# Hybrid layer stack on one core: where expert-table transfers stand among GpSimd's operations, and when the first late tiles' table rows are read

## The chip, the core and the metric

The kernel runs on one core of a Trainium2 chip. A core has five engines that run side by side, each in the order of its own instruction stream: TensorE (PE, matrix products; its weight loads are shown as PEld), VectorE (DVE), ScalarE (ACT), GpSimd (POOL) and SyncE (SP, which here only issues transfers). The engines wait for each other through semaphores. Transfers between the on-chip memory and DRAM run on 16 DMA engines; those whose rows are chosen by an index held on the chip (indirect transfers) are issued by GpSimd and occupy it for about a microsecond each, all others are issued by SyncE, in its order.

The metric is the device time of the core in microseconds, from the first instruction to the last.

## What is computed

Four layers follow each other on x, which is 2 batches of 2048 positions of 256 numbers in float32:

```python
x = L0_attn_a_u
x = x + _L0_attn_a_ref(_layernorm(x), ...)   # state space layer
x = x + _L0_ffn_ref(_layernorm(x), ...)      # experts
x = x + _L0_attn_b_ref(_layernorm(x), ...)   # attention
x = x + _L0_ffn_ref(_layernorm(x), ...)      # the same experts again
```

The state space layer, cut to what matters:

```python
zxbcdt = jnp.einsum('bld,ed->ble', u, W_in)
z = zxbcdt[..., :D_INNER]
xBC = zxbcdt[..., D_INNER:D_INNER + CONV_DIM]
dt = zxbcdt[..., D_INNER + CONV_DIM:]
xBC = jax.nn.silu(_causal_depthwise_conv(xBC, conv_w, conv_b))
x, Bm, Cm = ...                              # parts of xBC; x has 8 heads of 64
dt = jax.nn.softplus(dt + dt_bias)
A = -jnp.exp(A_log)
# for each position, per head: h = h * exp(dt * A) + (dt * x) B ; y = h C
y = _ssd_scan(dt, A, x, Bm, Cm)
y = y + D * x
y = y * jax.nn.silu(z)
y = y * lax.rsqrt(jnp.mean(y * y, axis=-1, keepdims=True) + EPS) * norm_w
return jnp.einsum('ble,de->bld', y, W_out)
```

The experts layer: each of the 4096 tokens is scored for 8 experts, the two with the highest scores are kept, and the token gets the weighted sum of those two experts' results:

```python
scores = x @ Wr.T + br
w = softmax(scores)
_, idx = jax.lax.top_k(scores + biases_N, 2)
val = w at idx, divided by its sum
h = x @ Wl1[e] + bl1[e]                      # a, b = halves of h, 512 wide each
y = (silu(a) * b) @ Wl2[e] + bl2[e]
out = sum over the two experts of val * y
```

## The kernel before

**Tiling.** The 4096 tokens are eight groups of 512 positions (`order`: the two batches in turn, place by place; a name such as f02 is the group of batch 0, place 2), and each group is four chunks of 128 (a name such as 021 is batch 0, place 2, chunk 1). The state space layer takes the 32 chunks in turn, and in each it carries the state h of the batch forward.

**Routing on the chip.** When a group's chunks are done, its tokens are scored and ranked (`prepare`), and each token gets two slots in a table in DRAM, one for each of its experts. A row of the table holds a token number, a weight and a second index. The rows are written by `enter` (L433): eight indirect transfers for each group (4 chunks by 2 experts), issued by GpSimd. Slots fill by expert, so that as soon as enough groups are entered some tiles of 256 rows of one expert are known to be full. `plan_early` works out on VectorE which those are. After groups 3, 4, 5, 6 and 7 it admits tiles up to number 5, 9, 13, 17 and 21 (`EARLY`), so that 21 "early" tiles, fe0 to fe20, are computed while the state space layer still runs. The rest, f0 and on, follow after it.

**An expert tile.** It reads its table rows (`rows`, tab_fe, L656, on SyncE), loads its expert's weights w1, w2, b1, b2 (`load`, L668 to L674, on SyncE; each has two buffers, so the load of a tile waits until the tile two before has done with them), gathers its 256 tokens (xs_fe, L683, indirect, GpSimd), transposes them (pxs_fe on PE, copied as xT_fe by ScalarE), makes four pieces of the up product (pab_fe, L722, 8 products each in two PSUM buffers; ScalarE applies silu, sa_fe L730, VectorE multiplies, gT_fe L731, which frees the PSUM buffer), the down product (pf_fe, L754), the weighting (y_fe, L767) and adds the result to the residual rows in DRAM by two indirect transfers (resid, L778, GpSimd).

**A chunk.** The loop body of the state space layer issues, for chunk i: a step of the early tile; `spread`, the load lb of chunk i+2's row of decays to all partitions (L1023, SyncE, two buffers); `chunk_front` of chunk i+1 (PE: pz, px, pb; ScalarE: eight operations lt that read lb, L1044, and an exponential; VectorE: dtx, xd, gm; GpSimd: wx L1071); a step of the early tile; `chunk_back` of chunk i (PE: py, ph, pi; GpSimd: h times its decay L1098, y+xd L1110, y*sz L1113, with VectorE's y, h+ph L1100 and y+pi L1112 between); a step of the early tile; and `chunk_out` of chunk i-1 (ScalarE: the square of y L1122; GpSimd: the inverse root ss L1124; PE: transposes pty, the output product po L1132; VectorE: x L1140). Between these stand pieces of the next group's projection (`project`: pc, pe, pd).

**Places of the transfers.** `late.step()` is called behind each of five GpSimd operations of a chunk: wx, h, y+xd, y*sz and ss. Each call lets the generator `entering` go on by one step: some empty steps, then one table transfer a step. `tc.issue_after(on_pool[0])` says that a transfer may not be issued before the GpSimd operation recorded last by `pool(...)`.

**Order.** A list scheduler of the framework decides the order of each engine's instructions in this stage [...], except for SyncE, which keeps the order of the program. So a transfer's lower bound is the operation it was called behind, and the scheduler may still put later operations of GpSimd ahead of it. In `run`, which does the tiles f0 and on, the orders of GpSimd, ScalarE and VectorE are also those of the program. After the last chunk a short loop goes on with the steps that are left, and then the late tiles begin; `fetch(tables, tiles)` reads table rows and loads weights up to the numbers given.

Of the kernel before, what the change touches and what calls it, by code (L numbers as in the profile page):

```python
# [8 lines left out]
F32 = mybir.dt.float32  # L9
# [4 lines left out]
P = 128  # L14
# [32 lines left out]
def kernel(  # L47
# [24 lines left out]
    nc = tc.nc  # L72
# [5 lines left out]
    fe = ctx.enter_context(tc.tile_pool(name="fe", bufs=2))  # L78
# [8 lines left out]
    order = [(b, s) for s in range(NS) for b in range(NB)]  # L87
# [139 lines left out]

    on_pool = []

    def pool(i):  # L230
        on_pool[:] = [i.ins]


    def layernorm(x, name):

        st = lnp.tile([P, GT, 6], F32, tag="st", name=f"st_{name}")
        mv = lnp.tile([P, GT, 2], F32, tag="mv", name=f"mv_{name}")
        for t in range(GT):
            nc.vector.bn_stats(st[:, t, :], x[:, t, :])
            nc.vector.bn_aggr(mv[:, t, :], st[:, t, :])  # L240
        yield
        rs = lnp.tile([P, GT], F32, tag="rs", name=f"rs_{name}")
        nc.vector.tensor_scalar(rs, mv[:, :, 1], EPS, None, ALU.add)
        pool(nc.gpsimd.tensor_tensor(rs, rs, mhalf, ALU.pow))
        yield
        xn = lnp.tile([P, GT, DM], F32, tag="xn", name=f"xn_{name}")
        for t in range(GT):
            nc.vector.tensor_scalar(
                xn[:, t, :], x[:, t, :], mv[:, t, 0:1], rs[:, t : t + 1], ALU.subtract, ALU.mult
            )  # L250
        return xn, rs, mv[:, :, 1]
# [24 lines left out]
    def apart(i, group, reason):  # L276
        tc.declare_no_dep(i.ins, group=group, reason=reason)
        tc.add_to_no_dep_group(group, i.ins)

    class Experts:  # L280
# [132 lines left out]
        def enter(self, pay, at, off):  # L413

            if self.rest is not None:
                rest, self.rest = self.rest, None
                for t in range(TT // P):
                    for e in range(NE):
                        with tc.issue_after(on_pool[0]):
                            i = nc.gpsimd.indirect_dma_start(  # L420
                                out=self.table,
                                out_offset=bass.IndirectOffsetOnAxis(ap=self.free[:, t, e : e + 1], axis=0),
                                in_=rest[:, t, :],
                                in_offset=None,
                            )
                        apart(i, f"free_{self.name}", "slots differ")
                        self.freed.append(i.ins)
                        if e % 2:
                            yield
            for t in range(GT):  # L430
                for c in range(2):
                    with tc.issue_after(on_pool[0]):
                        i = nc.gpsimd.indirect_dma_start(  # L433
                            out=self.table,
                            out_offset=bass.IndirectOffsetOnAxis(ap=at[:, t, c : c + 1], axis=0),
                            in_=pay[:, t, c, :],
                            in_offset=None,
                        )

                    apart(i, f"table_{self.name}", "slots differ")  # L440
                    for j in self.freed:
                        tc.add_manual_dep(
                            i.ins,
                            j.name,
                            mybir.DependencyInfo(mybir.DependencyClass.Sync, mybir.DependencyReason.DATA),
                            reason="behind the tokens that fill the first slots",
                        )
                    tc.declare_no_dep(i.ins, group=f"rows_{self.name}", reason="slots of full tiles are taken")
                    if c or not self.direct:
                        yield  # L450
# [403 lines left out]
    ffn = Experts("f", tc.dram_tile([NT + TT, DM], F32, name="resid"))  # L854
# [3 lines left out]
    with tc.tile_pool(name="ssm1", bufs=1) as s1, tc.tile_pool(name="ssm2", bufs=2) as s2:  # L858
# [170 lines left out]
        def chunk_front(b, s, t, g, lb):  # L1029
# [21 lines left out]
            for c in range(DI // P):  # L1051
# [17 lines left out]

            wx = s2.tile([P, DI], F32, tag="wx", name=f"wx_{nm}")  # L1070
            pool(nc.gpsimd.tensor_tensor(  # L1071
                wx.rearrange("p (h d) -> p h d", h=NH),
                dtxh,
# [7 lines left out]
        def chunk_back(b, s, t, g, f):  # L1081
# [14 lines left out]
            nc.tensor.matmul(ph, f["bt"], f["wx"], start=True, stop=True)  # L1096
            hh = h.rearrange("p (h d) -> p h d", h=NH)
            pool(nc.gpsimd.tensor_tensor(hh, hh, g["dec"][:, 1, t, :].unsqueeze(2).to_broadcast(per_head), ALU.mult))  # L1098
            late.step()
            nc.vector.tensor_tensor(h, h, ph, ALU.add)  # L1100
# [45 lines left out]
        late = Aside()  # L1146
# [6 lines left out]
        EARLY = {3: 5, 4: 9, 5: 13, 6: 17, 7: 21}  # L1153
# [3 lines left out]
        def routing(b, s):  # L1157
            nonlocal routed
            routed_group = yield from ffn.prepare(b, s, "B", known=True)
            routed += 1  # L1160
            late.add(entering(routed, routed_group))
            if routed + 3 < len(order):
                load_x(*order[routed + 3], x_rows(flat(u), *order[routed + 3]))


        def entering(n, group):
            if n < len(order):
                for _ in range(9 if 3 < n < len(order) - 1 else 4):
                    yield
            yield from ffn.enter(*group)  # L1170
            if n in EARLY:
                ffn.plan_early(n, EARLY[n], group[2])
# [32 lines left out]
        while late.waiting:  # L1205
            if not planned and len(ffn.seq) == EARLY[len(order) - 1]:
                ffn.plan()
                planned = True
            late.step()
            tiles.step()  # L1210
    ssm_w.__exit__(None, None, None)

    attw = ctx.enter_context(tc.tile_pool(name="attw", bufs=1))
# [3 lines left out]
    late = ffn.run()  # L1217
# [9 lines left out]
    with tc.tile_pool(name="att1", bufs=1) as a1, tc.tile_pool(name="att2", bufs=2) as a2:  # L1227
# [29 lines left out]
        EARLY = {4: 5, 6: 9}  # L1257
# [283 lines left out]
```

## Time and profile before

Times are of three runs; the profile is one more execution, whose records run over a span of 1694.1 us.

| | us |
|---|---|
| time, median of three runs | 1698.82 |
| lowest and highest | 1694.02, 1705.58 |
| profiled execution, its own time | 1695.92 |
| its span | 1694.1 |
| mean granted TensorE clock | 0.972 of full speed |

By its trace the profiled execution has these stretches:

| us from the start | what runs | PE busy, us |
|---|---|---|
| 0 to 140 | constants, first projections, first chunks | 118.53 |
| 140 to 262 | chunks; the transfers of the first two groups | 105.78 |
| 262 to 310 | chunks; the third group is entered and planned | 40.33 |
| 310 to 716 | chunks with one early expert tile beside each | 378.85 |
| 716 to 880 | late expert tiles | 159.12 |
| 880 to 920 | passage to the attention layer | 34.79 |
| 920 to 1320 | attention layer | 389.98 |
| 1320 to 1694 | experts again | 356.74 |

A stretch minus PE's busy time is what PE idled there; the waits of the trace say for what. The 64 table transfers were issued from 144.4 us to 697.6 us and took 1.13 us each on GpSimd, 72.3 us in all.

### The profile page before, as it was taken

How to read it: one execution, taken by the hardware profiler on the slowest of the kernel's cores; microseconds unless marked ns; L12 is line 12 of the kernel's file. 1: busy time of each engine (PE TensorE's matmuls, PEld its weight loads, DVE VectorE, ACT ScalarE, POOL GpSimd, SP SyncE). 2: the span in 40 equal slices, each digit the busy share in tenths (PEclk: the TensorE clock that was granted, in tenths of full speed). 3: DMA queues.
4: the chain of work that ended last, by engine and by line, in shares of the span. 5: the costliest groups of instructions: out<-in, count | busy, mean ns of one | idle time of the engine just before them, and what ended most of it. 6: DMA issues, size and time to landing. Idle time of an engine off the chain costs nothing.

```text
span 1694.1 us, 22151 instructions
## 1 busy us (share of the span) xinstructions
PE 1584.1 (94%) x7088; PEld 1193.8 (70%) x7088; DVE 897.0 (53%) x2471; ACT 670.9 (40%) x1338; POOL 736.2 (43%) x702
## 2 busy tenths in 40 slices
PE   6997988989989989999998999899999999999997
PEld 4664555677766777788885566475767878888886
DVE  6778878837648464422226757547554622222222
ACT  4886867856647543222332201101020322333322
POOL 2356357455555566634442002422240663544443
PEclk9898988999989999999999999999999999999999
DMA  4112202742535455889852231706435588888883
GB/s 157 38 54 60 88 28 61 215 126 61 168 63 160 125 144 131 209 244 320 230 133 82 54 72 52 100 13 139 144 62 150 147 215 240 222 231 229 230 215 48
DMA packets 174744, 231.30 MB, mean 137 GB/s; under 512 B 45920, under 2 KB 138080, under 8 KB 174368
## 3 DMA queue, kind: packets, MB, share of 16 engines
q1 hardware_dynamic: 143520, 193.42, 38.9%
q0 software_dynamic: 31104, 36.42, 12.0%
q8 instruction: 58, 0.95, 0.2%
q14 instruction: 62, 0.51, 0.1%
HBM read 192.72 MB, written 37.06 MB: 136 GB/s over the span
## 4 chain that ended last, share of the span: by engine, by line
PE 66%; DVE 12%; DMA 11%; POOL 5%; ACT 3%; issue 3%; SPq 1%; DVEq 0%; POOLq 0%; ACTq 0%
PE pab_g L722 9%; PE pao L1431 7%; PE pab_fe L722 5%; PE pq L1337 5%; PE pab_f L722 5%; PE pf_g L754 4%; PE pf_fe L754 4%; PE pab_ge L722 3%; DVE xc L1007 3%; PE pk L1337 3%; PE pvd L1411 3%; PE pi L1103 2%; DMA lb<-sums 2%; PE pc L990 2%; PE pf_f L754 2%
## 5 line engine op out<-in xcount | busy, mean ns | idle before, releaser
L722 PE MATMUL pab_g<-xT_g,w_g 128*128 128x256 f32 (+1 forms) x896 | 181.6, 361 | 0.0
L722 PE MATMUL pab_fe<-xT_fe,w_fe 128*128 128x256 f32 x672 | 157.8, 390 | 20.0 <-DVE gT_fe L731 17.1
L722 PEld LDWEIGHTS pab_g<-xT_g,w_g 128*128 128x128 f32 x896 | 158.5, 191 | 19.4 <-ACT xT_g L713 0.4
L722 PEld LDWEIGHTS pab_fe<-xT_fe,w_fe 128*128 128x128 f32 x672 | 128.5, 194 | 46.9 <-DVE gT_fe L731 21.8
L778 POOL DMA_INDIRECT out_dram<-y_g,tab_g x51 | 80.3, 1575 | 137.4 <-DVE y_g L767 57.9
L730 ACT ACTIVATE sa_g<-pab_g,b_g 128x256 f32<-128x256 f32 (+1 forms) x112 | 50.9, 454 | 191.3 <-PE pab_g L722 191.3
L731 DVE SCALAR_TENSOR_TENSOR gT_g<-pab_g,b_g,sa_g 128x256 f32<-128x256 f32 (+1 forms) x112 | 51.5, 460 | 129.0 <-ACT sa_g L730 129.0
L1337 PE MATMUL pq<-w_qkv_sb,axT 128*128 128x512 f32 x256 | 117.1, 597 | 0.0
L1007 DVE SCALAR_TENSOR_TENSOR xc<-pre,conv_w_sb,xc 128x512 f32<-128x512 f32 x144 | 113.3, 796 | 6.0 <-ACT xc L999 5.4
L1431 PE MATMUL pao<-w_o_sb,o 128*128 128x256 f32 x512 | 112.3, 380 | 0.0
L1431 PEld LDWEIGHTS pao<-w_o_sb,o 128*128 128x128 f32 x512 | 97.1, 190 | 15.8 <-issue 2.6
L433 POOL DMA_INDIRECT table_g<-pay_g,at_g x64 | 62.7, 980 | 86.2 <-DVE w_g L409 52.7
L990 PE MATMUL pc<-xT,w_in_sb 128*128 128x512 f32 x192 | 97.4, 638 | 0.4 <-ACT xc L999 0.4
L722 PE MATMUL pab_f<-xT_f,w_f 128*128 128x256 f32 (+1 forms) x512 | 96.6, 347 | 0.0
L754 PE MATMUL pf_g<-w_g,gT_g 128*128 128x256 f32 x408 | 92.9, 380 | 0.0
L722 PEld LDWEIGHTS pab_f<-xT_f,w_f 128*128 128x128 f32 x512 | 85.5, 191 | 9.4
L1044 ACT ACTIVATE lt<-lb,cum 128x128 f32<-128x128 f32 x256 | 82.8, 394 | 19.0 <-DMA lb<-sums 19.0
L1337 PEld LDWEIGHTS pq<-w_qkv_sb,axT 128*128 128x128 f32 x256 | 48.6, 192 | 58.8 <-issue 57.4
L1352 ACT ACTIVATE kd<-pk 128x512 f32<-128x512 f32 x32 | 19.1, 597 | 162.4 <-PE pk L1337 96.0
L778 POOL DMA_INDIRECT resid<-y_fe,tab_fe x42 | 67.0, 1595 | 37.5 <-DVE y_fe L767 21.9
L731 DVE SCALAR_TENSOR_TENSOR gT_fe<-pab_fe,b_fe,sa_fe 128x256 f32<-128x256 f32 x84 | 39.7, 480 | 80.5 <-ACT sa_fe L730 80.4
L754 PE MATMUL pf_fe<-w_fe,gT_fe 128*128 128x256 f32 x336 | 80.3, 392 | 2.2 <-DVE gT_fe L731 2.2
(477 smaller groups left out, 3368.6 us busy)
## 6 DMA issues: line engine op xcount, KB each, us to landing
w_g<-in_wl_dram SPq DMA_DIRECT2D x28, 1024.0 KB
w_fe<-in_wl_dram SPq DMA_DIRECT2D x21, 1024.0 KB
lb<-sums SPq DMA_DIRECT2D x32, 512.0 KB
w_f<-in_wl_dram SPq DMA_DIRECT2D x16, 1024.0 KB
o<-prob SPq DMA_DIRECT2D x32, 512.0 KB
w_g<-in_wl_dram SPq DMA_DIRECT2D x28, 512.0 KB
w_fe<-in_wl_dram SPq DMA_DIRECT2D x21, 512.0 KB
w_ge<-in_wl_dram SPq DMA_DIRECT2D x9, 1024.0 KB
```

Source lines behind the costliest of these rows:

```text
L433: i = nc.gpsimd.indirect_dma_start(out=self.table, out_offset=bass.IndirectOffsetOnAxis(ap=at[:, t, c : c + 1], axis=0), in_=pay[:, t, c, ...
L722: nc.tensor.matmul(p[:, q * n : (q + 1) * n], t["w1"][:, k, c * P : (c + 1) * P], t["xT"][:, k, :], start=(k == 0), stop=(k == KD - 1),)
L730: nc.scalar.activation(sa[:, :n], p[:, 0:n], AF.Silu, bias=t["b1"][:, i : i + 1])
L731: nc.vector.scalar_tensor_tensor(t["gT"][:, i, :n], p[:, n : 2 * n], t["b1"][:, NHT + i : NHT + i + 1], sa[:, :n], ALU.add, ALU.mult)
L754: nc.tensor.matmul(pos[h][:, h * DM : (h + 1) * DM], t["gT"][:, j, h * P : (h + 1) * P], t["w2"][:, j, :], start=(j == 0), stop=(j == NHT ...
L778: j = nc.gpsimd.indirect_dma_start(out=self.acc if self.direct else self.acc[: self.seq[i][4] or NT + TT, :], out_offset=bass.IndirectOffs ...
L990: nc.tensor.matmul(pc, w_in_sb[:, k, DI + c * P : DI + (c + 1) * P], xT[:, k, :], start=(k == 0), stop=(k == KD - 1),)
L1007: nc.vector.scalar_tensor_tensor(xc[:, c, :], pre[:, c, j : j + TG], conv_w_sb[:, c, j : j + 1], xc[:, c, :], ALU.mult, ALU.add,)
L1044: nc.scalar.activation(lt[:, i, :], lb[:, i, :], AF.Relu, bias=g["cum"][:, t, i : i + 1], scale=-1.0)
L1337: nc.tensor.matmul(p, src[:, k, t * P : (t + 1) * P], w_qkv_sb[:, k, j, half * TG : (half + 1) * TG], start=(k == 0), stop=(k == KD - 1),)
L1411: nc.tensor.matmul(pvd, w_qkv_sb[:, k, 2, c * P : (c + 1) * P], xd[:, k, :], start=(k == 0), stop=(k == KD - 1),)
L1431: nc.tensor.matmul(po[:, j * DM : (j + 1) * DM], o[i][:, c, (t + j) * P : (t + j + 1) * P], w_o_sb[:, c, :], start=(c == 0), stop=(c == NA ...
```

## The change

- **A fixed order on GpSimd.** Each table transfer is put into the list `in_table`. The next operation that goes through `pool(...)` is made to depend on it without a semaphore: it must stand behind it in GpSimd's stream. Together with the lower bound that was there, a transfer now stands just between two operations of the program's order. `enter` of the second experts layer (`direct`) takes no part.
- **Other holds.** `entering` waited 9 empty steps for groups 4 to 6 and 4 for groups 1, 2, 3 and 7, and none for group 8. It now waits 5, 5, 4 and 1 for groups 4, 5, 6 and 7, 3 for groups 1 to 3, and none for group 8.
- **The loop after the last chunk** takes two late steps a turn where it took one, each followed by a one-number memset on GpSimd that goes through `pool(...)`, so that the transfers have operations to stand behind.
- **Table rows of late tiles.** `fetch(25, 0)` is called at the end of the state space stage: SyncE reads the rows of the first late tiles' table (tab_f0 and on) before it loads the weights of the last early tile.

```diff
@@ pool
     on_pool = []
+    in_table = []
 
     def pool(i):
         on_pool[:] = [i.ins]
+        while in_table:
+            tc.add_manual_dep(
+                i.ins,
+                in_table.pop().name,
+                mybir.DependencyInfo(mybir.DependencyClass.NoSync, mybir.DependencyReason.DATA),
+                reason="transfers into a table keep their order",
+            )
@@ Experts.enter
                             in_=pay[:, t, c, :],
                             in_offset=None,
                         )
+                    assert self.direct or not in_table
+                    in_table.append(i.ins)
@@ entering
+        HELD = {4: 5, 5: 5, 6: 4, 7: 1}
+
         def entering(n, group):
             if n < len(order):
-                for _ in range(9 if 3 < n < len(order) - 1 else 4):
+                for _ in range(HELD.get(n, 3)):
                     yield
             yield from ffn.enter(*group)
@@ after the last chunk
             late.step()
+            pool(nc.gpsimd.memset(fe.tile([P, 1], F32, tag="sep", name="sep"), 0.0))
+            late.step()
+            pool(nc.gpsimd.memset(fe.tile([P, 1], F32, tag="sep", name="sep"), 0.0))
             tiles.step()
+        ffn.fetch(EARLY[len(order) - 1] + 4, 0)
     ssm_w.__exit__(None, None, None)
```

By the instruction orders of the two programs, a transfer stands at every one of the five places in the new one as well. TensorE, VectorE and ScalarE get a new order in the state space stage too, since the scheduler works from the new constraints: an early tile's up and down products move by a third to half a chunk against the chunk's own products. The attention layer and the second experts layer keep their orders but for a few places.

## The prediction

> **What bounds the kernel now.** I read the page first (busy shares and slices), then busy time by stretch, then the waits of the stretch that holds most of the change, then the chain of waits inside it. The page names TensorE:
>
> ```profile
> PE 1584.1 (94%) x7088; PEld 1193.8 (70%) x7088; DVE 897.0 (53%) x2471; ACT 670.9 (40%) x1338; POOL 736.2 (43%) x702
> ```
>
> GpSimd, whose order is changed, is 43% busy, so its work costs only where somebody waits for it. Busy time by stretch says where that can be; the change touches the first three rows and the first microseconds of the fourth:
>
> ```profile
> 140.00:262.00 122.00, 105.78 (x463) 68.67 (x464) 100.33 (x249) 87.39 (x172) 68.50 (x63) 0.90 0.20 57
> 262.00:310.00 48.00, 40.33 (x182) 27.07 (x180) 39.53 (x112) 34.09 (x71) 33.02 (x31) 0.89 0.26 69
> 310.00:716.00 406.00, 378.85 (x1757) 294.44 (x1757) 239.36 (x703) 218.61 (x431) 223.54 (x197) 0.97 0.51 138
> 716.00:880.00 164.00, 159.12 (x832) 141.34 (x833) 43.11 (x98) 49.91 (x114) 71.54 (x57) 0.99 0.84 244
> ```
>
> The columns are stretch and length, busy PE, weight loads, DVE, ACT, POOL, the granted clock, DMA share and GB/s. PE is idle 16.2, 7.7, 27.2 and 4.9 us. In the first two stretches DVE is nearly as busy as PE, so a delay there reaches PE through DVE. From 310 on one early expert tile (fe) runs beside each chunk, and PE alone is the bound. Its waits there, and those of the engines that feed it (us, times, longest):
>
> ```profile
> PE pab_fe L722 <- DVE gT_fe L731: 17.1, 13, 4.3
> PE pxs_fe L709 <- DMA xs_fe<-xnd_f,tab_fe: 3.8, 3, 1.6
> ACT lt L1044 <- DMA lb<-sums: 19.0, 9, 4.6
> ACT yt L1122 <- POOL y L1113: 45.0, 14, 5.6
> SPq L670 <- PE pf_fe L754: 58.5, 13, 6.5
> SPq L656 <- DMA table_f<-pay_f,at_f: 20.0, 5, 5.0
> ```
>
> Two thirds of PE's idle time is an up pass (pab) waiting for a PSUM buffer that DVE's gT has not freed. The chain of waits shows why (start, duration, what):
>
> ```profile
> 326.88 3.45 PE pf_fe L754 x16
> ...
> 331.92 6.22 DMA lb<-sums
> 338.14 0.02 issue
> 338.16 0.69 ACT lt L1044 x2
> 338.85 0.36 ACT sa_fe L730
> ...
> 475.15 8.76 DMA lb<-sums
> 483.91 0.02 issue
> 483.93 0.03 ACT lt L1044
> 483.96 0.28 issue
> 484.24 1.26 ACT lt L1044 x4
> 485.50 0.37 ACT sa_fe L730
> 485.87 0.03 issue
> 485.89 0.49 DVE gT_fe L731
> ```
>
> SyncE's queue holds the load of the next tile's w2 (L670) until this tile's down pass (pf_fe) has read the old one; the chunk's row broadcast lb stands behind it, lands 6 to 9 us later, and ScalarE, which works in order, stands on lt with sa_fe behind it. So the kernel's loss in its longest stage is the phase between a tile's down pass and the next chunk's lb.
>
> **The change part by part.** All 64 table transfers stay: their row (64 instructions, 72.3 us on POOL, 1.13 us each) is the same before and after.
>
> 1. Holds. A group's eight transfers began after 9 late steps for groups 4 to 6 and 4 for the others; now after 5, 5, 4 (groups 4, 5, 6), 1 (group 7), else 3. By the instruction orders of the two programs they stand up to one chunk earlier on POOL. What waits for them is SyncE's read of table rows: 20.0 us in 5 waits, on a queue with lb behind it. They now come ahead of lb, rather than after: 2 to 5 us each, most of it under other loads' waits.
>
> 2. Program order on POOL. Each transfer now stands between the two POOL operations of its place. It adds no POOL time, but wx, h, y+xd, y*sz or ss behind it start 1.13 us later each. At 140 to 262 POOL shows 68.50 us in 122 and its transfers are already mixed with the chunk's operations: I take 0, bounds -3 and +3 (half the 6.4 us that DVE waits there for h).
>
> 3. The first early tile. Its last transfer came at 293.7 by the trace, its table read at 298.9, its rows landed at 310.6. With the new hold I put the last transfer some 10 us earlier, and the read at about 289, behind the planning on DVE (about 4 us) that must precede it. In the new order the tile's transposes (pxs_fe0) stand before the following chunk's py, so PE waits there about 4.5 to 6 us instead of 1.05; the stage still ends earlier: -3, bounds -9 and +3.
>
> 4. The steady part, where the scheduler's order follows. An early tile moves by a third to half a chunk: its down pass now precedes py, ph and pi, where it closed the chunk before. So w2's slot comes free half a chunk earlier relative to the use of lb, and the waits on lb should go: at most the 17.1 us of PE waits, if nothing takes their place. What is late next: in the new order POOL has both scatter-adds of a finished tile (2 x 1.60 us, the resid row) ahead of h, y+xd and y*sz, and ACT has the square of y (L1122, waits for y*sz) ahead of the next sa_fe in ten passes. In a pass with three transfers POOL then runs wx 1.04, scatter-adds 3.19, h 1.18, y+xd 1.41, y*sz 1.31 and transfers 3.4 = 11.5 us in series, without transfers 8.1. PE's own work in a pass that projects nothing is pz 1.73, pab 6.9, pf 3.5, pi 1.73, py, ph 0.87 each, po 1.8, transposes 1.65, so 19.05 us, where the down passes are 20.6 to 22.1 apart. Walked engine by engine with these durations, a pass without transfers comes to 19.8 to 20.3: -0.5 to -1 in fe6, 7, 10 and 11, together -3. In fe2, from the end of the down pass before: y_fe 0.5, scatter-adds 3.19, h and a transfer 2.31, y+xd and a transfer 2.54, DVE's y+pi 0.69, y*sz 1.31, then ACT's square 0.82, sa_fe 0.45 and gT 0.48 make 12.3, while PE has py, ph, pi 3.47, transposes 0.88, half of pz 0.87, two up pieces 3.45 and po 1.8, so 10.5: it waits 1.8, and with some 3 us of POOL's backlog from the pass before, which I estimate from the chunk's two earlier transfers and a late y_fe, 4.9. So passes with transfers: fe2 +3.4, fe3 +1.4, fe12 0, fe13 -1.9, fe14 +2.3, and fe4, 5, 8, 9 -1 to 0, together +3. I take 0 for the stage, bounds -17 (all waits gone) and +20 (a wait of 2 us in each of the ten passes).
>
> 5. Table rows of tab_f0 to 3 before the late tiles. They were asked for at 717.92, behind the last early tile's weights, and PE waited 1.62 us for the rows at 729.81, after 0.7 for a transpose. Asked for about 10 us sooner, the gather still needs the slot that fe19's transposes free (715.4) and stands between scatter-adds on POOL, so it gains 1.5 to 2.2: -2, bounds -3 and 0.
>
> 6. Ten memsets on POOL in the drain: 0.11 to 0.70 us each by the sep rows, beside a PE that does not wait for POOL there: 0; if the cover fails, +3.
>
> Sum: 0 - 3 + 0 - 2 + 0 = -5 on the profiled execution, 1695.92 us (span 1694.1), which is 2.9 below the median of 1698.82. So 1694.
>
> **A rule weighed.** The granted clock falls after idle PE. In steps of 5 us:
>
> ```profile
> 380.00:385.00 5.00, 3.73 (x10) 3.00 (x11) 3.25 (x5) 4.95 (x11) 2.85 (x2) 0.70 0.00 0
> 485.00:490.00 5.00, 3.57 (x8) 2.86 (x9) 3.25 (x5) 4.95 (x11) 2.78 (x2) 0.50 0.00 0
> ```
>
> Ahead of the second PE had idled 4.3 us, ahead of the first only 2.5. [...] By the row at 380, a wait of 2.5 us too costs 0.3 x 5 = 1.5 us. [...] I take the rule for the two long waits on one side and the dip at 485 that goes on the other: even, within the sum. By the row on all four it would be +3.
>
> **The rivals.** A, slower: the wait on lb is replaced by one on POOL. ACT stands at the square of y until y*sz is done, sa_fe and gT come late, and PE waits in the up pass. For it: ACT already waits 45.0 us there, 14 times, and POOL's 11.5 us in series fill more than half a pass. Against: DVE and PE have half a chunk to spare in passes without transfers. It decides if y*sz ends after the next tile's second up piece; then some ten passes lose 2 us and four of them a dip of 1.5: +26, so 1721.
>
> B, faster: POOL keeps up, and the lb waits (17.1) go with the two dips after them (1.5 + 2.5) and parts 3 and 5: -21 to -25, less what single transfers still cost: 1676. For it: PE's work of 19.05 us leaves 1.5 us or more per pass to win. Against: the square ahead of sa_fe.
>
> C, the change does not do what it says: no line limits transfers to two places, the step still stands at all five, and the order of the new program has transfers at each of them. If so, and the scheduler's new order only exchanges waits, 1697 to 1700.
>
> **How the numbers follow.** About 1% is what a measurement of this kernel can tell from no change: under 1682 or over 1716. Forecast 0.50 (1684 to 1706), A 0.28 (1710 to 1732), B 0.14 (1668 to 1682), C 0.08. Faster: B and the forecast's edge, 0.15. Slower: four fifths of A, 0.22. Same: 0.63. The range 1672 to 1724 leaves out B's lower third and A's upper third, about a tenth and a half.
>
> **What would show it.** PE's waits for gT in 310 to 716 under 17.1 and ACT's waits for lb under 19.0 confirm part 4; ACT's wait for y*sz above 45.0 with sa_fe behind it is A. The first pxs_fe before 310.6 confirms part 3, the first tab_f row read before 717.9 and no wait for xs_f confirm part 5. Down passes 20 us apart where no transfer stands, and 22 or more where three do, fit the forecast. I am wrong if the attention stage or the last one changes by more than 2 us: their order hardly moves.

## The result: 2.8% slower, and the profile after

The changed kernel takes 1747.93 us (median of 6 runs, 1745.51 to 1750.26), the kernel before 1701.12 (6 runs beside it): a ratio of 1.0281, 95% interval 1.0261 to 1.0301. Its profiled execution spans 1746.5 us where that of before spans 1694.1, so 52.4 more. I forecast 1694 with a range to 1724.

The page says first of what kind the loss is: TensorE's 7088 products are the same, but it is busy 1596.1 us where it was busy 1584.1. Those 12.0 us go with a lower granted clock (a mean of 0.962 after 0.972); the other 40.4 are idle time.

Cut at the ends of the first and of the last early tile's down pass, the 52.4 us lie as follows: 8.6 before the first (330.3 us becomes 338.9), 28.0 between them (410.55 becomes 438.58), 15.8 after the last. The first two together, 36.6 us, are the loss of the state space stage, called the 36 us below. Busy time by stretch of the kernel after, first two stretches at the times that were shown of before, the third between those two tiles (columns as there):

```profile
140.00:262.00 122.00, 102.72 (x451) 67.90 (x451) 91.15 (x238) 82.31 (x172) 65.60 (x61) 0.90 0.19 57
262.00:310.00 48.00, 36.11 (x140) 24.75 (x139) 34.63 (x100) 26.67 (x57) 28.60 (x28) 0.75 0.16 51
338.90:777.48 438.58, 390.83 (x1806) 304.47 (x1806) 233.38 (x682) 210.30 (x417) 233.26 (x217) 0.96 0.50 132
```

The third of them in the kernel before:

```profile
330.30:740.85 410.55, 381.75 (x1785) 298.93 (x1784) 226.71 (x649) 208.05 (x411) 231.44 (x202) 0.98 0.53 140
```

TensorE idles 47.8 us instead of 28.8 in the third, and works 9.1 us longer, partly on 21 more products, as the chunks now run behind the tiles, partly at the lower clock. In the second the clock fell from 0.89 to 0.75. The waits of the kernel after, in the third stretch:

```profile
ACT yt L1134 <- POOL y L1125: 55.7, 12, 7.6
PE pab_fe L734 <- DVE gT_fe L743: 23.9, 8, 6.2
ACT lt L1056 <- DMA lb<-sums: 7.7, 2, 4.0
PE pk_f L373 <- DVE sel_f L367: 6.9, 3, 3.4
DVE xn_a L258 <- POOL rs_a L254: 6.4, 2, 3.2
```

The wait for lb did fall, from 19.0 to 7.7. Yet TensorE's wait for gT rose from 17.1 us in 13 waits to 23.9 in 8: fewer and longer. The two longest have the same pattern. This is the timeline around the longest one (start, duration, engine, what; in brackets the idle time before and what ended it), some lines left out:

```profile
392.84 1.28 POOL L1125 TENSOR_TENSOR y<-y,sz 128x512 f32<-128x512 f32 x1
...
394.29 1.00 POOL L443 DMA_INDIRECT table_f<-pay_f,at_f  x1 [0.17 <-issue]
...
395.32 0.57 POOL L1136 TENSOR_TENSOR ss<-ss,mhalf 128x1 f32<-128x1 f32 x1
...
396.08 1.04 POOL L443 DMA_INDIRECT table_f<-pay_f,at_f  x1 [0.19 <-issue]
397.15 1.04 POOL L254 TENSOR_TENSOR rs_a<-rs_a,mhalf 128x4 f32<-128x4 f32 x1
...
398.23 1.38 DVE L258 TENSOR_SCALAR xn_a<-x,mv_a,rs_a 128x256 f32<-128x256 f32 x4 [3.17 <-POOL rs_a L254]
...
399.95 0.45 DVE L743 SCALAR_TENSOR_TENSOR gT_fe<-pab_fe,b_fe,sa_fe 128x256 f32<-128x256 f32 x1
...
400.45 5.84 PE L734 MATMUL pab_fe<-xT_fe,w_fe 128*128 128x256 f32 x16 [6.18 <-DVE gT_fe L743]
```

rs_a is the inverse root of the layer normalisation of the group that is projected next. It goes through `pool(...)` too (L254), so the fixed order puts it behind the transfers called before it. VectorE stands 3.17 us on xn_a, which needs rs_a, and has gT queued behind it; ScalarE's sa_fe was done at 395.8. (So the first 1.5 us of TensorE's 6.18, up to 395.8, were for sa_fe, which stood behind the square of y; the rest was for VectorE.) TensorE stands in the middle of an up pass, and the granted clock falls there as well, to 0.79 and then to 0.52 (last column but two):

```profile
395.00:400.00 5.00, 0.00 (x0) 0.00 (x0) 1.79 (x10) 4.97 (x12) 3.45 (x5) 0.79 0.03 2
400.00:405.00 5.00, 4.55 (x11) 3.70 (x12) 2.09 (x8) 2.05 (x3) 0.00 (x0) 0.52 0.00 0
```

**After the last early tile.** A correction is due to the section on the change: it says that `enter` of the second experts layer takes no part. The diff says otherwise. The assertion only lets that layer have several transfers in the list; they are appended in both layers. In the second layer's entry the same thing happens as above, with eight transfers and two scatter-adds ahead of rs_g. The timeline of the kernel after:

```profile
1372.65 0.99 POOL L443 DMA_INDIRECT table_g<-pay_g,at_g  x1 [0.30 <-issue]
1373.95 0.97 POOL L443 DMA_INDIRECT table_g<-pay_g,at_g  x1 [0.30 <-issue]
1374.94 1.05 POOL L254 TENSOR_TENSOR rs_g<-rs_g,mhalf 128x4 f32<-128x4 f32 x1
1376.03 1.40 DVE L258 TENSOR_SCALAR xn_g<-x,mv_g,rs_g 128x256 f32<-128x256 f32 x4 [8.85 <-POOL rs_g L254]
...
1377.35 0.86 DVE L743 SCALAR_TENSOR_TENSOR gT_ge<-pab_ge,b_ge,sa_ge 128x256 f32<-128x256 f32 x2
...
1377.86 2.50 PE L766 MATMUL pf_ge<-w_ge,gT_ge 128*128 128x256 f32 x5 [7.38 <-DVE gT_ge L743]
```

Before, rs_g went ahead of the transfers:

```profile
1317.54 1.01 POOL L244 TENSOR_TENSOR rs_g<-rs_g,mhalf 128x4 f32<-128x4 f32 x1 [15.72 <-DVE offs_g L366]
```

From the end of one second-layer tile's down pass to that of the next, 21.9 us pass there, and 13.0 in the kernel before: 8.8 of the 15.8.

### The profile page after: what moved, and what is told of

It is laid out like the page before. It is cut to its first block, busy times and chain, and to the rows that moved or that the text cites. A ratio compares the mean times of both kernels' runs of the same rounds, so it can differ in the third digit from the quotient of the medians.

```text
span 1746.5 us, 22157 instructions
## 1 busy us (share of the span) xinstructions
PE 1596.1 (91%) x7088; PEld 1202.9 (69%) x7088; DVE 893.2 (51%) x2471; ACT 662.6 (38%) x1332; POOL 738.5 (42%) x712
## 4 chain that ended last, share of the span: by engine, by line
PE 62%; POOL 10%; DVE 10%; DMA 8%; issue 6%; ACT 2%; SPq 0%; DVEq 0%; POOLq 0%; ACTq 0%
PE pab_g L734 9%; PE pao L1449 6%; PE pq L1355 5%; PE pab_fe L734 5%; PE pab_f L734 5%; PE pf_g L766 4%; PE pc L1002 3%; PE pvd L1429 3%; PE pk L1355 3%; PE pab_ge L734 3%; PE pf_fe L766 2%; POOL table_f L443 2%; DMA o<-prob 2%; DMA out_dram<-y_g,tab_g 2%; DVE xc L1019 2%
## 5 line engine op out<-in xcount | busy, mean ns | idle before, releaser
L734 PE MATMUL pab_fe<-xT_fe,w_fe 128*128 128x256 f32 x672 | 163.8, 400 | 28.3 <-DVE gT_fe L743 24.1
L734 PEld LDWEIGHTS pab_fe<-xT_fe,w_fe 128*128 128x128 f32 x672 | 133.1, 201 | 60.6 <-DVE gT_fe L743 29.0
L1083 POOL TENSOR_TENSOR wx<-dtx,dec 128x512 f32<-128x512 f32 x32 | 33.3, 1042 | 131.1 <-DVE dtx L1068 131.0
L1115 PEld LDWEIGHTS pi<-dtx,lt 128*128 128x128 f32 x512 | 68.7, 212 | 21.0 <-DVE y L1101 13.1
L766 PEld LDWEIGHTS pf_g<-w_g,gT_g 128*128 128x128 f32 x408 | 75.6, 191 | 9.2 <-DVE gT_g L743 0.2
## 6 DMA issues: line engine op xcount, KB each, us to landing
o<-prob SPq DMA_DIRECT2D x32, 512.0 KB, 14.6
```

The source lines that it names most:

```text
L734: nc.tensor.matmul(p[:, q * n : (q + 1) * n], t["w1"][:, k, c * P : (c + 1) * P], t["xT"][:, k, :], start=(k == 0), stop=(k == KD - 1),)
L766: nc.tensor.matmul(pos[h][:, h * DM : (h + 1) * DM], t["gT"][:, j, h * P : (h + 1) * P], t["w2"][:, j, :], start=(j == 0), stop=(j == NHT ...
L1115: nc.tensor.matmul(pi[:, i * HD : (i + 1) * HD], f["lt"][:, i, :], f["dtx"][:, i * HD : (i + 1) * HD], start=True, stop=True,)
```

## The experiments

Each time is a median; behind it stands the ratio to the kernel before, run beside it, with its 95% interval in brackets. The median of the kernel before lay between 1698.69 and 1704.79 us. Where a share is given "by the ratios", the difference of two ratios is taken times 1700 us.

### Which part of the change

**The order, in the first layer alone**

```diff
-                    assert self.direct or not in_table
-                    in_table.append(i.ins)
+                    if not self.direct:
+                        in_table.append(i.ins)
```

> The changed kernel with table transfers of the second experts layer left out of the list, so that only the first layer's transfers keep a fixed place. Theory L (in the second layer the list holds the inverse root of the last group's normalisation, rs_g13, behind eight transfers, and DVE and PE stand for it): about 11 us under the changed kernel, so 1735 to 1739, the wait of pf_ge for gT_ge of 7.4 us gone and rs_g13 ahead of its transfers again. Rival (the 11 us at that place are an accident of when transfers meet there, as everything arrives 36 us later): no gain, 1746 to 1750.

1740.86 us, 1.0232 (1.0163 to 1.0300). By the ratios it is 8 us under the changed kernel, though the two intervals overlap; the second-layer tile takes 13.0 us again, and TensorE's waits in the first layer are the same (23.9 us, 8, 6.2). To see the second layer by itself, the reverse on the kernel before (`if self.direct:` ahead of the append, nothing else changed):

> The kernel before with the order fixed for the transfers of the second experts layer and nowhere else. From the profile of the changed kernel (a tile step of 21.8 us there where the others take 13.0): 7 to 11 us slower than before. Rival (it needs the changed kernel's arrival times): within 3 us.

1713.52 us, 1.0045 (1.0027 to 1.0064), so 7.7 us, clear of its interval; the tile step is 23.1 us there. Both runs give the second layer's share as 7 to 8 us of the 48, with no need of the changed kernel's arrival times.

**The holds alone**, on the kernel before, those of groups 4 to 7 (groups 1 to 3 stay at 4):

```diff
-                for _ in range(9 if 3 < n < len(order) - 1 else 4):
+                for _ in range({4: 5, 5: 5, 6: 4, 7: 1}.get(n, 4)):
```

> The kernel before with the new holds for groups 4 to 7 (5, 5, 4, 1; groups 1 to 3 keep 4) and nothing else. Theory O (the fixed order on GpSimd costs the 36 us of the state space stage): the holds alone change little, 1690 to 1710. Rival H (the earlier transfers shift the early tiles against the chunks, and that costs it): most of the 36 us, 1725 to 1740.

1705.42 us, 1.0010 (0.9988 to 1.0031): no difference.

**The order alone**: the first run with the holds of before and without the early `fetch`.

> The changed kernel with the holds of before (9 and 4), the order fixed in the first experts layer alone, and no early read of table rows. Theory O: slower than before by 25 to 40 us, 1725 to 1740, with GpSimd's h and rs_a behind transfers and DVE waiting for them. Rival H: within 10 us of before.

1712.22 us, 1.0048 (1.0026 to 1.0069). I expected 25 to 40 us, and there are 8. In its trace the first early tile is 8.0 us late, 1 us is added over the next 19, and 5.5 us at the last one. So neither half makes the loss of 36 us by itself; it needs both. That threw over both theories as I had put them.

**The early table read alone** (`ffn.fetch(...)` added to the kernel before):

> The kernel before with the early read of the late tiles' table rows and nothing else. My prediction's part 5: 1.5 to 3 us faster, 1696 to 1699, with the wait of pxs_f for xs_f (4.2 us in 2 waits) down to under 2. Rival (the gather stands behind scatter-adds, or the row reads hold up the last tile's weights): no difference or up to 3 us slower.

1702.26 us, 0.9974 (0.9943 to 1.0004). This run taught something else. Its instruction order turned out to be that of before on all five engines: with one late step a turn, all early tiles' loads have been issued by then, and `run` reads those rows next anyway. So it is the same program twice (the twin, below), and tells how far apart two measurements of one program can lie: 0.3% in the ratio, and 1694.1 and 1701.0 us in the profiles, of which the part behind the last early tile differs by 8.2 us. A loss or gain of that size in one profile's late part is not evidence here, and a ratio within 0.3% of 1 is little by itself. Up to the last early tile the traces agree better: the first tile ends at 330.3 and 327.2 us in the two, and the stretch from there to the last takes 410.5 and 412.3. With the changed loop, of two late steps a turn, the early read does matter: without it (the run before) the last early tile ends 19.1 us after the one before it, with it 12.9 (in the run below with group 3 held for 4 steps), and 13.5 in the kernel before.

### The phase

Comparing the new orders showed what the two halves share. Held 3 steps instead of 4, group 3's plan is ready one tile step sooner in the program's order (not in time, as will be seen). The first tile then begins at the second of a chunk's three places for tile steps and not at the third, and the tiles keep that phase: in the kernel before, each down pass beside a chunk closes it, behind its py, ph and pi; now it stands ahead of pi, and in most tiles ahead of py and ph too. So I took phase and holds apart in three runs.

**Group 3 held for 4 steps** (and with it groups 1 and 2): the first run with `HELD.get(n, 4)`.

> The kernel with the order fixed in the first layer alone (the first run), but groups 1 to 3 held for 4 steps as before; groups 4 to 7 keep 5, 5, 4 and 1. Its instruction order has the down pass of a tile after py, ph and pi again, as before the change. Theory P (one step less of hold for group 3 sets the first tile half a chunk apart from the chunks, and this phase costs the 28 us between the first and the last early tile): the 28 us go, 1705 to 1717. Rival Q (the earlier transfers of groups 4 to 7 cost it): 1730 to 1742.

1705.61 us, 1.0045 (1.0027 to 1.0062). By the ratios one step of hold is worth 32 us. **The mirror**, 3 steps for groups 1 to 3 and the old 9, 9, 9, 4 for the rest:

> The mirror of it: the order fixed in the first layer alone, groups 1 to 3 held for 3 steps, groups 4 to 7 held for 9, 9, 9 and 4 as before. Theory P: the phase is the changed kernel's, and so is the loss, 1732 to 1745. Rival Q: 1705 to 1717.

1751.21 us, 1.0316 (1.0283 to 1.0349): all of the loss and more (with the tables late, TensorE also waits 12.7 us for gathered rows). **All new holds, the first tile's start moved** by one place:

```diff
-            tiles.step()
+            if ffn.next[1]:
+                tiles.step()
             aside.step(3)
             y = chunk_back(b, s, t, groups[b, s], this)
```

> The kernel with the order fixed in the first layer alone and all the new holds (the first run, 1740.9 us), with one edit: the first early tile may not take its first step at the second of a chunk's three places for tile steps, so it begins one place later. From the third tile on its TensorE order has the phase of the kernel before. Theory P (the phase of tiles against chunks, which one step of hold shifted, makes the 28 us): 1703 to 1715, like the run with group 3 held for 4. Rival (the earlier table of group 3 itself, by its transfers or plan among the chunk's work): 1730 to 1742.

1717.79 us, 1.0077 (1.0053 to 1.0102): 26 us of the loss go by the ratios, with no hold touched; its interval just meets that of the run with group 3 held for 4. Now **the phase without the order**: the kernel before, its first tile allowed to start at the second place only.

> The kernel before with its own holds and no fixed order, and the first early tile allowed to begin only at the second of the three places, so that the down passes stand ahead of pi and pty, close to the changed kernel's phase. If the phase costs by itself: the tiles begin up to two thirds of a chunk later and the steady stage is longer, 1720 to 1740. If it costs only together with transfers fixed between GpSimd's operations (rs behind them): 1698 to 1712.

1698.89 us, 0.9972 (0.9955 to 0.9989). Its order comes close to the changed kernel's without being the same: the down passes stand ahead of pi, but in more tiles than there behind py or ph. The ratio is no gain, as the twin gave 0.9974. So this phase costs nothing where the scheduler may put GpSimd's operations ahead of transfers, and the loss needs both, the phase and the fixed order. One combination was not run: all the new holds in the shifted phase without the fixed order.

### Which fixed operation

**rs free**: the changed kernel, all holds and both layers as they are, but the inverse root may pass the transfers.

```diff
-    def pool(i):
+    def pool(i, free=False):
         on_pool[:] = [i.ins]
-        while in_table:
+        while in_table and not free:
...
-        pool(nc.gpsimd.tensor_tensor(rs, rs, mhalf, ALU.pow))
+        pool(nc.gpsimd.tensor_tensor(rs, rs, mhalf, ALU.pow), free=True)
```

> The changed kernel, except that the inverse root of a normalisation (rs, L254) may go ahead of the transfers called before it; all other operations of GpSimd keep the fixed order, in both layers. Theory R (rs behind the last transfers of a group holds DVE, which has gT behind it: PE waits of 6.2 and 5.5 us in the first layer and 7.4 us in the second, each followed by half clock): 1715 to 1728. Rival P alone (phase and scatter-adds make the waits): the gain of the second layer alone, 1737 to 1743.

1716.54 us, 1.0124 (1.0085 to 1.0163): by the ratios 27 of the 48 us go by that one operation, and the phase is still the shifted one. (The scheduler plans anew with rs free, so the two kernels differ in other places of their orders too.) The profiles say where: the first early tile ends at 331.1 us instead of 338.9, 7.8 less; the stretch from there to the last takes 428.0 instead of 438.6, 10.6 less; the second layer's tile step is 13.0 instead of 21.9, 8.9 less. That is 27.3 in all. The stretch between the tiles with rs free:

```profile
331.09:759.08 427.99, 387.43 (x1796) 302.25 (x1796) 227.04 (x676) 208.21 (x415) 231.92 (x216) 0.96 0.51 135
```

So of the 28.0 us that this stretch lost, rs explains 10.6, and 17.5 stay. What is gained ahead of the first tile is gained before 262 already, where rs_a stands behind the last transfers of the first and the second group. In the changed kernel TensorE waits 5.6 and 4.0 us there ahead of the transposes of xn_a (pt_a); the first of these waits:

```profile
160.39 1.05 POOL L254 TENSOR_TENSOR rs_a<-rs_a,mhalf 128x4 f32<-128x4 f32 x1
...
162.88 0.48 PE L267 MATMUL pt_a<-ident,xn_a 128*128 128x128 f32 x1 [5.57 <-DVE xn_a L258]
```

With rs free these two roots run at 120.3 and 180.6 instead of 160.4 and 226.4, and one wait of 2.4 us is left ahead of pt_a. Then the complement, the first run with **h, y+xd and y*sz free** and rs, wx and ss fixed, and after it both free:

> The kernel with the order fixed in the first layer alone (the first run, 1740.9 us), except that h, y+xd and y*sz may pass the transfers called before them; rs, wx and ss may not. Its phase is the shifted one. Theory R (rs makes most of the loss): 1728 to 1741, with the waits of 6.2 and 5.5 us before the third and seventh tile's up passes still there. Rival Y (the transfers between h, y+xd and y*sz delay the square and with it sa_fe and gT): 1705 to 1718.

> The same, with rs free as well: only wx and ss keep their place behind the transfers. If rs and the chain of y are the whole loss, each for a part: 1698 to 1708. If the phase together with wx and ss, or with the scatter-adds alone, makes the rest: 1712 to 1722, like the run with the roots free.

1737.74 us (1.0205, 1.0138 to 1.0272) and 1716.59 us (1.0071, 1.0052 to 1.0090). Freeing h and the chain of y gains nothing clear by itself; freeing rs too gains 23 us by the ratios. The waits of the run with h and y free, then of that with rs free (shifted phase in both):

```profile
PE pab_fe L734 <- DVE gT_fe L743: 17.1, 6, 5.4
DVE xn_a L258 <- POOL rs_a L254: 6.4, 2, 3.2
```

```profile
PE pab_fe L734 <- DVE gT_fe L743: 10.6, 7, 2.8
PE pe L980 <- DVE gT_fe L743: 4.3, 1, 4.3
PE pe L980 <- DVE da L973: 4.1, 1, 4.1
DVE h L1112 <- POOL h L1110: 23.4, 8, 3.8
PE pk_f L373 <- DVE sel_f L367: 5.8, 2, 3.9
```

With rs free, VectorE's wait for rs_a is gone from the list, and no wait of an up pass for gT is longer than 2.8 us. TensorE's longest waits are now others for VectorE, at pe and pk_f (4.3, 4.1 and 3.9 us). What is left in this phase, 0.7 to 1.2% or the 17.5 us above, stays open. VectorE's wait for h is a candidate (20.5 us in the changed kernel, 1.7 in the kernel before), but h was free to pass in the last run and its wait did not go (23.1 us), so the runs do not show it.

Why the same wait costs less in the other phase is seen with group 3 held for 4. Its waits from the first to the last early tile, and its timeline at rs:

```profile
PE pab_fe L734 <- DVE gT_fe L743: 10.8, 12, 2.5
DVE xn_a L258 <- POOL rs_a L254: 6.4, 2, 3.2
```

```profile
372.63 3.67 PE L766 MATMUL pf_fe<-w_fe,gT_fe 128*128 128x256 f32 x16
...
377.01 1.02 PE L1049 MATMUL pz<-w_in_sb,xT 128*128 128x512 f32 x2
...
377.87 1.94 PE L1144 MATMUL po<-w_out_sb,yt 128*128 128x264 f32 x8
378.06 1.04 POOL L443 DMA_INDIRECT table_f<-pay_f,at_f  x1 [0.18 <-issue]
379.13 1.06 POOL L254 TENSOR_TENSOR rs_a<-rs_a,mhalf 128x4 f32<-128x4 f32 x1
380.22 1.06 DVE L258 TENSOR_SCALAR xn_a<-x,mv_a,rs_a 128x256 f32<-128x256 f32 x3 [3.18 <-POOL rs_a L254]
...
382.16 5.38 PE L734 MATMUL pab_fe<-xT_fe,w_fe 128*128 128x256 f32 x16 [2.35 <-issue]
```

rs stands behind the transfers here too, and VectorE waits the same 6.4 us. But the down pass is over, no gT is queued behind xn_a, and TensorE has pz and po to do. It then idles 2.35 us ahead of the next up pass, for which the trace names no engine, and 2.0 us at the other rs_a (for xT_fe), instead of 6.2 and 5.5. From the first to the last early tile this run takes 403.8 us, the kernel before 410.5.

**Both repairs**, rs free and group 3 held for 4:

> Both together: rs free of the transfers, groups 1 to 3 held for 4 steps, order fixed in the first layer, groups 4 to 7 at 5, 5, 4, 1, table rows of the late tiles asked for sooner. If phase and rs are the whole loss and the early read keeps its 2 us: 1694 to 1704, so no slower than before. If the transfers between h, y+xd and y*sz cost by themselves: 1708 to 1720.

1705.24 us, 1.0056 (1.0036 to 1.0076). They do not add up: in the old phase it makes no difference that the ratios can tell whether rs is fixed (1.0045) or free. About half a per cent or a little more stays in every run with the first layer's order fixed, the old phase and nothing else added, hardly more than the twin's 0.3%; in each the first tile ends 4 to 8 us late by its profile, but in the run with group 3 held for 4 the last tile ends 0.6 us early by its profile, so where this half per cent lies is not settled.

### A version faster than both

The prediction's reading of the chain of waits (lb stuck behind w2 in SyncE's queue) can be tested on the kernel before, by issuing lb ahead of the tile step:

```diff
+            if i + 2 < len(chunks):
+                lbs[i + 2] = spread(*chunks[i + 2])
             tiles.step()
             this = front
-            if i + 2 < len(chunks):
-                lbs[i + 2] = spread(*chunks[i + 2])
```

> The kernel before with one move: the load lb of chunk i+2 is issued ahead of the tile step that issues the next tile's weight loads, so SyncE no longer holds it behind w2. My reading of the chain of waits (17.1 us of PE waits start from lb): 1684 to 1692, with the wait of lt for lb under 6 us. If another wait takes its place: 1695 to 1705.

1691.29 us, 0.9926 (0.9895 to 0.9957), faster than before by 0.7%. That is more than the 0.3% of the twin, and the profile shows it where it was expected: from the first to the last early tile 393.7 us pass, where the kernel before and its twin took 410.5 and 412.3. The waits fall as read, from 19.0 and 17.1 us:

```profile
ACT lt L1044 <- DMA lb<-sums: 1.9, 2, 1.0
PE pab_fe L722 <- DVE gT_fe L731: 2.5, 5, 0.8
```

By its profile the last early tile ends at 721.2 us, 19.7 before that of the kernel before. The same move on the kernel with group 3 held for 4, and together with the later start:

> The same move on the kernel with the order fixed in the first layer, groups 1 to 3 held for 4 and the other new holds (1705.6 us, half a per cent over before). If the lb wait is the loss there too: 10 us less, 1692 to 1699, which would be under before; if the fixed order has used up that slack: 1702 to 1708.

> The kernel before with lb issued ahead of the tile step (0.9926 of before) and the first early tile beginning only at the second place (0.9972). If they win on different waits: 0.988 to 0.992 of before. If both remove the same wait on lb: 0.992 to 0.995, and over that if the one spoils the other.

1702.13 us (0.9989, 0.9968 to 1.0009) and 1699.84 us (0.9979, 0.9960 to 0.9999). The first is half a per cent better than without the move, but no better than before. In the second the move gains nothing beside the later start alone (0.9972): ScalarE still waits 10.1 us for lb, as it waited 10.9 without the move. So the gain belongs to the old phase, which I had not expected.

## Why the prediction was wrong, step by step

**What bounds the kernel** was right: TensorE through lb and gT, as the moved lb shows with its 0.7%.

**The step that failed** is the list in part 2 of what can stand behind a transfer: wx, h, y+xd, y*sz or ss. The inverse root rs goes through `pool(...)` as well and is not on it, so parts 2, 3 and 4 put at nothing what VectorE, and TensorE behind it, wait for rs. Freeing rs alone took away 27 of the 48 us.

**Part 4** has a second failure. I saw the phase shift of the early tiles in the instruction orders, and that the lb wait would shrink with it (19.0 to 7.7). I priced the part at 0; it measures +28.0, beyond my bound of +20. rs makes 10.6 of this. The other 17.5 lie inside my bounds, but not at my 0: they need the shifted phase and the fixed order together, and which operation makes them is not known. Rival A had the sign, at 1721, and named the chain from y*sz over the square of y to sa_fe. Freeing h, y+xd and y*sz gained nothing clear, so that chain was not the main one, though the first 1.5 us of the longest wait are its. One wait of its kind is in the trace (4.3 us at 370.7 in the third tile, behind two scatter-adds and two gathers); with h and y free 2.3 us of it were left.

**Part 1** was right that the holds of groups 4 to 7 by themselves are worth nothing (1.0010). It did not see that the one step less for group 3 sets the phase, worth 32 us where the order is fixed. I expected SyncE to stand 2 to 5 us for table rows each time; it stood 98.3 us in 5 waits, the longest 32.4. That it isn't the cause is shown by the mirror run, with 14.4 us there and the larger loss.

**Part 2**: I took 0 for the stretch from 140 to 262, with -3 as the better bound. The output product of the chunk that ends at 261.9 us ended 3.8 us sooner, and with rs free it ended at 247.3, 14.6 us sooner. So the new order was worth far more here than my bound, and rs took most of it away again.

**Part 3** had the wrong sign: -3, and +8.6 measured, of which some 3 us can be the difference of two traces of one program. The last transfer did come sooner, though at 288.6 instead of 293.1 (the prediction has 293.7), and not by some 10 us. rs_a was behind it, VectorE stood 3.0 us on xn_a, and the plan, on VectorE too, was done at 301.6 instead of 297.9 us. The row read began at 302.6, not 289. TensorE waited 5.96 us up to 294 for VectorE, and the clock of that stretch fell to 0.75. That this root makes the delay is not shown: with rs free it stands behind the last transfer of this group too (at 277.3, and VectorE waits 3.0 us). That run's first tile is 7.8 us sooner because its chunks are, as said under part 2.

**Part 5** (-2) can't be seen: with the loop unchanged the read moves nothing, and with the loop changed it repairs what the loop would lose. **Part 6** (0) holds as far as a profile shows: from the 17th to the 20th tile the loss stays at 36.7 to 36.9.

**The late stages** I had said would not change by more than 2 us. The last one lost 8.8 in one tile, by rs again, through my misreading of `enter`; the other 7 of the 15.8 are within what two profiles of one program differ by.

**The rule weighed.** I took what the granted clock loses as even within the sum, and counted two long waits (in fe2 and ahead of pxs_fe0). In the stretch of the early tiles there were five, of 4.3, 6.2, 3.4, 5.5 and 3.4 us, each met by 3.4 or 6.8 us at half clock. The time at half clock rose there from 20.5 to 34.1 us; by my estimate from these two figures that can cost half of the difference, 6.8 us, at most. My count by the row at 380, where a wait of 2.5 us was met by half clock, is not refuted: one of 2.6 us at 663 was met by 3.4 us of it in this trace too. But a wait of 2.8 us at 638 was met by none (1.00 from 637 to 642), and one dip of 3.4 us, at 534, had no wait of that size ahead of it. Whether the length of a wait decides it is therefore not shown, and what a shorter wait costs is left open.

## What to carry to other kernels

When an order is fixed on an engine, list every operation that goes through the same helper, in all stages that use it, and ask of each who waits for it and what is queued behind that waiter: here, freeing a root of one microsecond took away more than half of a 2.8% loss. Where two loops are interleaved, a shift of a step is a change of phase, and the same wait of VectorE went with 2 us of idle TensorE in one phase and 6 us in another; so measure an order and a phase apart and together. And a load that a later stage needs soon should be issued ahead of the loads that wait for a buffer: with lb behind w2 in SyncE's queue ScalarE waited 19.0 us for it, with lb ahead 1.9 us. The move gained 0.7% in one phase and nothing in the other.

## What the runs showed of the hardware

In the clock records of the two profiles, of the kernel before and of the kernel after, the granted clock is either full (1.00) or half (0.50). The stretches at half in the kernel after last 3.41, 6.83, 10.24 and 17.07 us, those in the kernel before 3.41, 6.83 and 10.24 (the last record of each trace, which its end cuts off, is left out). By the mean clock, 2 x (1 - 0.9724) x 1694.1 = 94 us of the kernel before ran at half, 2 x (1 - 0.9618) x 1746.5 = 133 us of the kernel after. In the stretch of early tiles it was 34.1 us after and 20.5 before. In the version with lb ahead, the longest wait of TensorE in that stretch was 1.9 us, and the mean granted clock over its 393.67 us was 1.00.
